# Softmax denominators of a convolution-attention layer: sums by accumulating DMAs, reciprocals with queries on partitions, stacking through DRAM

## The chip, the cores and the metric

The kernel runs on one core of one Trainium2 chip. The core has five engines that run their own instruction streams: PE (TensorE, matmuls and transposes), DVE (VectorE), ACT (ScalarE), POOL (GpSimd) and SP (SyncE, which here only issues DMAs). They share an on-chip memory of 128 partitions (SBUF), a small memory into which PE writes (PSUM), and 16 DMA engines. The metric is the device time of one execution in microseconds. Before the change the median of three runs is 3320.81 us (3317.92 to 3323.6).

## What is computed

Two layers work on x of shape 8 x 256 x 32 x 32 in float32. Layer 0 is a convolutional attention block with a feed-forward part, layer 1 a causal attention with a mixture of experts. The change lies in the attention of layer 0. For each of 8 images, with N = 1024 pixels and 4 heads with 32 channels in q and k and 64 in v:

```
qkv = _bn(_conv1x1(_ln(x), qkv_w))
q, k, v = qkv.reshape(B, NH, 2*KD + HD, N) split along the channels
attn = softmax(einsum('bhkn,bhkm->bhnm', q, k) * SCALE, axis=-1)
out  = einsum('bhdm,bhnm->bhdn', v, attn)
out  = out + _bn(_dwconv3(v))          # depthwise 3x3
x    = x + gamma1 * _bn(_conv1x1(out, proj_w))
x    = x + gamma2 * edffn(_ln(x))      # 1x1, depthwise 3x3, gelu gate, 1x1, 8x8 spectral filter
```

## The kernel before

Layer 0 keeps channels on partitions. The loop at the end of layer 0 runs over the images, one iteration for each. `together` takes two generators: `main_of(i)`, the attention of image i with the norms, the spectrum of image i-2 and the queries, keys and values of image i+1 woven in; and, beside it, `hidden(i-1)`, the depthwise convolutions of the image before, whose nine taps are mostly DVE instructions (`tap`). Every generator yields an estimate of its microseconds, and `together` takes steps of the second as long as its sum is behind the first's. So the order of the instructions on each engine is fixed when the program is built. All engines are wrapped by `InOrder` (line 69), which keeps that order; therefore nearly all instructions carry line 69 in the profile and are told apart by the tiles that they write and read.

`attend` (attention proper) computes transposed scores, keys on partitions. For a chunk c of QC = 256 queries and a key tile j of 128 keys, four chunks of eight steps each per image:

- PE writes the scores of four heads into `s` from the stacked keys `kst` and queries `qst`. A stack holds 4 x 32 rows per head: q and k are split into a part `hi`, rounded to a short mantissa for PE's faster float32 form (F32R), and the rest `lo`, and the rows are (hi, lo, hi, lo) for q and (hi, hi, lo, lo) for k.
- ACT takes the exponential into `pT` (128 keys x 4 heads x 256 queries, 512 KB), which has two buffers.
- One step later `product` multiplies with the transposed values `vT` into `po`: eight matmuls of 32 output columns each. Four more matmuls with `ones` add the exponentials over the keys into `sums` (the tile `sm`), which holds every head's sum on 32 partitions.

`close` ends a chunk. ACT copies `po` and the sums to SBUF (`pu`, `ss`), and a list of steps is run by `later`, one in each of the following steps: DVE takes the reciprocal of 128 x 256 (`sr`), ACT and POOL split it into `rh` and `rl`, four matmuls with `pick_r` spread it over the 64 channels of each head into `rb`, and DVE multiplies and adds to `o`. After the last chunk `finish` runs the same list, woven into `values` of the next image.

`queries_keys` makes `hi` and `lo` of queries (g = 0) and keys (g = 1), a pair of tiles for each; `stack` copies them into `qst` and `kst` with 32 DMAs of 128 KB from SP's queue (line 680), when the last scores of the image before have been taken. `values` and `project` run during that time. `rms_norm` sums squares on PE, then a chain of seven small POOL instructions takes the inverse root (`a`, `y`, `r`), PE transposes it (`tr`) and spreads it with `pick_n` (`rbn`).

The tiles `vpad` and `hpad` hold images with a border of zeros, 34 rows of 34. `vec` holds all per-channel vectors of both layers and is loaded by the first DMA. `accs` collects a check sum of the sums and reciprocals, by which the program decides at its end whether a safe form of layer 0 (`layer0_shifted`) has to be run; with these inputs it isn't.

PSUM is full: `ps_s` holds two buffers of `s` (four banks), `ps_o` one `po` and one `sums`, `ps_m` two buffers that all other products share.

Of the kernel before, what the change touches and what calls it, by code (L numbers as in the profile page):

```python
# [9 lines left out]
F32 = mybir.dt.float32  # L10
F32R = mybir.dt.float32r
# [7 lines left out]
P = 128  # L19
# [33 lines left out]
for _name, _w in _VEC:  # L53
    _VOFF[_name] = (_n, _w)
    _n += _w
NVEC = _n


# [16 lines left out]
def conv_attn_hybrid_kernel(  # L75
# [29 lines left out]

    vec = const.tile([P, NVEC], F32, name="vec")
    nc.sync.dma_start(vec, vecs)

    def col(name, i=0, n=1):
        o, w = _VOFF[name]  # L110
        assert i + n <= w
        return vec[:, o + i : o + i + n]

# [318 lines left out]
    with ExitStack() as l0:  # L432
# [3 lines left out]
        ps_s = l0.enter_context(tc.tile_pool(name="ps_s0", bufs=2, space=PSUM))  # L436
        ps_o = l0.enter_context(tc.tile_pool(name="ps_o0", bufs=1, space=PSUM))
        ps_m = l0.enter_context(tc.tile_pool(name="ps_m0", bufs=2, space=PSUM))
# [72 lines left out]
        for k in range(KC):  # L511
# [7 lines left out]

        pick_r = wpool.tile([P, NH // 2, P], F32R, name="pick_r")  # L520
        pickr = one.tile([P, NH, HD], F32, tag="full", name="pickr", bufs=2)
        nc.gpsimd.memset(pickr, 0.0)
        nc.gpsimd.affine_select(
            out=pickr, in_=pickr, compare_op=ALU.not_equal, fill=1.0, base=0,
            pattern=[[-KD, NH], [0, HD]], channel_multiplier=1,
        )
        nc.gpsimd.tensor_copy(pick_r.rearrange("p a (b c) -> p (a b) c", c=HD), pickr)

        nq = HALF // P
        pick_n = wpool.tile([2 * nq, nq, P], F32R, name="pick_n")  # L530
        pickn = one.tile([2 * nq, nq, P], F32, tag="full", name="pickn", bufs=2)
        nc.gpsimd.memset(pickn, 0.0)
        for half in range(2):
            nc.gpsimd.affine_select(
                out=pickn, in_=pickn, compare_op=ALU.not_equal, fill=1.0, base=-nq * half,
                pattern=[[-1, nq], [0, P]], channel_multiplier=1,
            )
# [8 lines left out]
        def padded(name):  # L546
            p = one.tile([P, H + 2, W + 2], F32, tag=name, name=name)
            nc.gpsimd.memset(p, 0.0)
            return p

        vpad = [padded(f"vpad{i}") for i in range(KC)]
        hpad = [padded(f"hpad{i}") for i in range(2)]

        def interior(p, h):
            r = H // 2
            return p[:, 1 + h * r : 1 + (h + 1) * r, 1 : 1 + W]

# [3 lines left out]
        def tap(dst, p, w, k):  # L561
            src = p[:, k // 3 : k // 3 + H, k % 3 : k % 3 + W]
            dve.scalar_tensor_tensor(rows(dst), src, w[:, k : k + 1], rows(dst), ALU.mult, ALU.add)
# [5 lines left out]
        def rms_norm(b, wname, xn):  # L569
# [38 lines left out]
            def apply(h):  # L608
                rT = rT_of.pop(h)
                rb = ps_m.tile([P, HALF], F32, tag="mm", name="rbn")  # L610
                for i in range(nq):
                    pe.matmul(rb[:, i * P : (i + 1) * P], pick_n[:, i, :], rT, start=True, stop=True)
# [39 lines left out]
        def queries_keys(b):  # L652

            att[b] = {"xn": one.tile([P, KC, N], F32, tag="xn", name="xn")}
            yield from rms_norm(b, "n1w", att[b]["xn"])
            for g in range(2):  # L660
                hi = one.tile([P, N], F32R, tag=f"hi{g}", name="hi")
                lo = one.tile([P, N], F32, tag=f"lo{g}", name="lo")
                bias = qkv_o[:, g : g + 1]

                def take(hs, pq):
                    act.activation(hi[:, hs], pq, AF.Identity, bias=bias)
                    dve.scalar_tensor_tensor(lo[:, hs], pq, bias, hi[:, hs].bitcast(F32), ALU.add, ALU.subtract)

                yield from qkv_group(b, g, take)
                att[b][g] = (hi, lo)  # L670

        def stack(b):
            for g in range(2):
                hi, lo = att[b][g]
                name = ("qst", "kst")[g]
                att[b][name] = st = one.tile([P, NH, N], F32R, tag=name, name=name)
                for r in range(4):
                    src = (hi, lo, hi, lo)[r] if g == 0 else (hi, hi, lo, lo)[r]
                    for hd in range(NH):
                        nc.sync.dma_start(  # L680
                            st[r * KD : (r + 1) * KD, hd, :].bitcast(F32), src[hd * KD : (hd + 1) * KD, :].bitcast(F32)
                        )

# [30 lines left out]
        def v_conv(b):  # L714
            o = att[b]["o"] = one.tile([P, KC, N], F32, tag="o", name="o")
            for g in range(KC):
                mid = vpad[g][:, 1 : 1 + H, 1 : 1 + W]
                act.activation(rows(o[:, g, :]), mid, AF.Identity, bias=pe_o[:, g : g + 1], scale=pe_w[:, g, 4:5])
            for g in range(KC):
                for k in OTHERS:  # L720
                    tap(o[:, g, :], vpad[g], pe_w[:, g, :], k)
                    yield 1.3

        def attend(b):
# [6 lines left out]

            def product(po, sm, j, pT):


                for pair in range(NH // 2):
                    for i in range(4):
# [7 lines left out]
                        )  # L744
                for hd in range(NH):
                    pe.matmul(
                        sm[hd * KD : (hd + 1) * KD, :], ones[:, :KD], pT[:, hd, :], start=(j == 0), stop=(j == nj - 1)
                    )

            def close(c, po, sm):  # L750
                pu = two.tile([P, NH // 2, QC], F32, tag="pu", name="pu", bufs=1)
                act.copy(pu, po)
                ss = two.tile([P, QC], F32, tag="ss", name="ss", bufs=1)
                act.activation(ss, sm, AF.Copy, accum_out=accs[:, 0, b, c : c + 1])
                r = two.tile([P, QC], F32, tag="sr", name="sr", bufs=1)
                rh = two.tile([P, QC], F32R, tag="rh", name="rh", bufs=1)
                rl = two.tile([P, QC], F32R, tag="rl", name="rl", bufs=1)
                qs = slice(c * QC, (c + 1) * QC)

                def invert():  # L760
                    dve.reciprocal(r, ss)

                def split():
                    act.activation(rh, r, AF.Copy, accum_out=accs[:, 1, b, c : c + 1])
                    pool.tensor_sub(rl, r, rh.bitcast(F32))
# [19 lines left out]
            for c in range(N // QC):  # L785
                qs = slice(c * QC, (c + 1) * QC)
                po = ps_o.tile([P, NH // 2, QC], F32, tag="po", name="po")
                sm = ps_o.tile([P, QC], F32, tag="sm", name="sums")
                for j in range(nj):
                    ks = slice(j * P, (j + 1) * P)  # L790
                    s = ps_s.tile([P, NH, QC], F32, tag="s", name="s")
                    for hd in range(NH):
                        pe.matmul(s[:, hd, :], kst[:, hd, ks], qst[:, hd, qs], start=True, stop=True)
                    pT = two.tile([P, NH, QC], F32, tag="pT", name="pT")
                    act.activation(pT, s, AF.Exp)
                    if late:
                        product(*late[:4])
                        if late[2] == nj - 1:
                            todo = close(c - 1, *late[:2])
                    late = (po, sm, j, pT)  # L800
                    later()
                    yield 1.75
            product(*late)
            todo = close(c, po, sm)
            att[b]["rest"] = todo
# [49 lines left out]
        def group_on_pe(b, n):  # L855
# [15 lines left out]
            for h in range(2):  # L871
                pc = ps_m.tile([P, HALF], F32, tag="mm", name="pc")
                for k in range(9):
                    r0 = h * r + k // 3
                    pe.matmul(
                        pc, diag[:, k, :], pad[:, r0 : r0 + r, k % 3 : k % 3 + W], start=(k == 0), stop=(k == 8)
                    )
                act.copy(dst[:, h * HALF : (h + 1) * HALF], pc)
# [911 lines left out]
```

## Time and profile before

| | |
|---|---|
| median of three runs | 3320.81 us |
| the profiled execution, time | 3326.09 us |
| the profiled execution, span | 3324.3 us |
| PE busy | 3108.8 us (94%) |
| DVE busy | 2395.9 us (72%) |
| ACT busy | 1417.6 us (43%) |
| POOL busy | 328.9 us (10%) |
| mean granted PE clock | 0.969 |
| layer 0 | 0 to about 1455 us |
| layer 1, attention | about 1455 to 2090 us |
| layer 1, experts | about 2090 to 3324 us |

The profile's slices show each engine's share in 40 pieces of 83 us, a digit for each. The groups of instructions give, for one operation on one set of tiles, the number of instructions, their busy time together, the mean of one in ns, and the idle time of the engine just ahead of them with what ended it. Instructions of PE overlap, so a group's busy time is smaller than count times mean. An fp32 matmul counts as two instructions, one in F32R as one. The windows give the busy time of each engine in a stretch of the execution.

### The profile page before, as it was taken

Reading aid. Unit: us, or ns where it says so; the run is one execution under the profiler, and the core shown is the slowest. Engines: PE = TensorE matmul, PEld = TensorE weight load, DVE = VectorE, ACT = ScalarE, POOL = GpSimd, SP = SyncE. Lnnn points to the kernel's source line nnn. Section 1 sums busy time; section 2 is a strip of 40 time slices with the busy share of each in tenths; the row PEclk is TensorE's granted clock in tenths of the full one; section 3 lists DMA queues with packets and bytes.
Section 4 is the critical chain, followed back from the end, with each engine's and each line's share of the span. In section 5 each row is a group of like instructions: output and inputs, shape, how many; then the busy total and the mean of one; then the engine's idle time right before and its main releaser. Section 6 shows DMA issues by size and latency. Waiting matters only on the chain.

```text
span 3324.3 us, 43278 instructions
## 1 busy us (share of the span) xinstructions
PE 3108.8 (94%) x17366; PEld 2108.0 (63%) x17366; DVE 2395.9 (72%) x3710; ACT 1417.6 (43%) x2185; POOL 328.9 (10%) x530
## 2 busy tenths in 40 slices
PE   6998999999999998769999998999999999999999
PEld 4554646464656555345556666687878777878787
DVE  2369788878787887744554444688888877888887
ACT  2545454555454544313333332344444444444443
POOL 1120101020202010001222222400000000000000
PEclk9989999999999999879999999899999999999999
DMA  4112020202020200030111101100000000000000
GB/s 121 29 24 51 26 52 26 51 27 51 27 51 26 52 14 7 16 134 13 51 47 43 39 26 45 45 25 21 20 20 20 24 18 26 23 20 26 13 7 13
DMA packets 42918, 113.85 MB, mean 34 GB/s; under 512 B 6406, under 2 KB 14550, under 8 KB 38870
## 3 DMA queue, kind: packets, MB, share of 16 engines
q1 hardware_dynamic: 42710, 111.01, 11.0%
q8 instruction: 139, 2.28, 0.3%
q14 instruction: 69, 0.57, 0.1%
HBM read 43.61 MB, written 33.82 MB: 23 GB/s over the span
## 4 chain that ended last, share of the span: by engine, by line
PE 50%; DVE 4%; ACT 1%; POOL 1%; issue 0%; DMA 0%; POOLq 0%; ACTq 0%; SPq 0%; DVEq 0%
PE pm L69 12%; PE pa L69 12%; PE q L69 11%; PE s L69 5%; PE po L69 3%; PE pv L69 2%; PE pk L69 2%; DVE zt L69 1%; DVE nm L69 1%; PE tpt L69 1%; DVE pr L69 1%; PE tp L69 1%; ACT pr L69 1%; PE tpz L69 1%; PE pw L69 1%
## 5 line engine op out<-in xcount | busy, mean ns | idle before, releaser
L69 ACT ACTIVATE h<-h,bn_o,bn_s 128x512 f32<-128x512 f32 x384 | 308.7, 813 | 632.5 <-DVE h L69 632.4
L69 DVE SCALAR_TENSOR_TENSOR conv<-hpad,vec,conv 128x1024 f32<-128x1024 f32 x256 | 331.4, 1300 | 14.7 <-ACT conv L69 8.9
L69 DVE SCALAR_TENSOR_TENSOR x<-hpad,vec,x 128x1024 f32<-128x1024 f32 x248 | 321.6, 1300 | 23.5 <-ACT x L69 17.4
L69 ACT ACTIVATE pT<-s 128x1024 f32<-128x1024 f32 x256 | 261.6, 1024 | 150.3 <-PE s L69 150.1
L69 PE MATMUL pm<-h,w 128*128 128x512 f32 (+1 forms) x768 | 318.1, 523 | 0.0
L69 PE MATMUL po<-pT,vT 128*32 128x256 f32 x4096 | 276.5, 388 | 6.5 <-ACT pT L69 4.8
L69 PE MATMUL ph<-xn,piw 128*128 128x512 f32 x512 | 246.1, 608 | 3.1 <-DVE gf L69 1.1
L69 PE MATMUL s<-kk,z 128*128 128x512 f32 x512 | 242.4, 601 | 0.6 <-DVE pr L69 0.6
L69 PE MATMUL s<-qst,kst 128*128 128x256 f32 x1024 | 217.9, 335 | 6.1 <-DMA kst<-lo 5.9
L69 PEld LDWEIGHTS s<-qst,kst 128*128 128x128 f32 x1024 | 147.8, 192 | 88.8 <-issue 72.2
L69 PEld LDWEIGHTS pm<-h,w 128*128 128x128 f32 x768 | 146.7, 191 | 75.6 <-issue 62.1
L69 DVE TENSOR_TENSOR h<-h,wb 128x1024 f32<-128x1024 f32 x128 | 156.8, 1225 | 43.2 <-ACT h L69 43.2
L69 DVE TENSOR_TENSOR h<-pa,first 128x512 f32<-128x512 f32 x128 | 88.3, 690 | 134.9 <-PE pa L69 131.4
L69 DVE SCALAR_TENSOR_TENSOR o<-vpad,pe_w,o 128x1024 f32<-128x1024 f32 x128 | 163.3, 1281 | 24.1 <-ACT o L69 21.2
L69 ACT ACTIVATE hpad<-ph,pi_o 128x512 f32<-128x512 f32 x126 | 87.0, 691 | 211.7 <-PE ph L69 207.2
L69 DVE TENSOR_TENSOR h<-h,first 128x256 f32<-128x256 f32 x384 | 164.3, 428 | 13.2
L69 PEld LDWEIGHTS po<-pT,vT 128*32 128x32 f32 x4096 | 107.7, 109 | 88.7 <-ACT pT L69 8.3
L69 PEld LDWEIGHTS ph<-xn,piw 128*128 128x128 f32 x512 | 90.8, 190 | 108.9 <-issue 92.1
L69 PE MATMUL sums<-pT,ones 128*32 128x256 f32 x2048 | 158.8, 382 | 0.0
L69 PE MATMUL pz<-pow__118,hid 128*128 128x256 f32 x512 | 129.8, 408 | 29.1 <-DVE hid L69 29.1
L69 PE MATMUL pa<-tz,ws 128*128 128x256 f32 x512 | 156.0, 387 | 0.0
L69 PE MATMUL pa<-ze,w 128*128 128x256 f32 x512 | 153.8, 383 | 0.0
(258 smaller groups left out, 5940.3 us busy)
## 6 DMA issues: line engine op xcount, KB each, us to landing
t<-in_x_dram SPq DMA_DIRECT2D x8, 1024.0 KB, 7.5
qst<-hi SPq DMA_DIRECT2D x64, 128.0 KB, 2.3
qst<-lo SPq DMA_DIRECT2D x64, 128.0 KB, 2.3
kst<-hi SPq DMA_DIRECT2D x64, 128.0 KB, 2.3
kst<-lo SPq DMA_DIRECT2D x64, 128.0 KB, 2.3
td<-t SPq DMA_DIRECT2D x8, 1024.0 KB, 3.8
t<-td SPq DMA_DIRECT2D x8, 1024.0 KB, 4.9
ze<-zd SPq DMA_DIRECT2D x16, 512.0 KB, 4.1
```

The lines of the kernel that those rows point to most:

```text
L69: return self._tc.keep_in_program_order(method(*args, **kwargs))
```

## The change

Four things change in layer 0, and some tiles get smaller.

1. `product` has no matmuls with `ones` any more. The exponentials of key tile 0 are written to a new tile `acc` in place of `pT`; those of each later tile are added to `acc` by a DMA that POOL issues with an adding operation. `pT` has three buffers and `acc` two. After the last tile, `total` makes the sums of a chunk with four matmuls on `acc`.
2. `close` no longer copies `po` to SBUF at once; `po` has two buffers. The sums are transposed (`turn`), so that queries lie on partitions and a reciprocal has 128 x 2 x 4 elements; POOL splits it into two parts (`rs`), PE transposes it back (`back`), two matmuls spread it (`spread`), ACT copies it to `pu`, and DVE multiplies with `po` (`divide`).
3. `hi` and `lo` have one buffer each for q and k together. SP writes them to DRAM (`part`) as soon as they are complete, and `stack` reads each stack with four DMAs from there, eight of 512 KB for an image in place of 32 of 128 KB.
4. `vec` is loaded in two parts, the second (`vec2`, the vectors of the experts) behind layer 0. `vpad` and `hpad` have rows of 33 elements, so that one column of zeros serves as the right border of a row and the left border of the next. `pick_n` is 8 x 4 and is widened by a stride of 0 in the matmul; `pick_r` is made for eight rows.

```
-        ps_o = l0.enter_context(tc.tile_pool(name="ps_o0", bufs=1, space=PSUM))
+        ps_o = l0.enter_context(tc.tile_pool(name="ps_o0", bufs=2, space=PSUM))
...
+            p = one.tile([P, (H + 2) * (W + 1) + 2], F32, tag=name, name=name)
...
+        def inside(p, r0, c0, h):
+            o = r0 * (W + 1) + c0
+            return p[:, o : o + h * (W + 1)].rearrange("p (h w) -> p h w", w=W + 1)[:, :, :W]
...
-                hi = one.tile([P, N], F32R, tag=f"hi{g}", name="hi")
-                lo = one.tile([P, N], F32, tag=f"lo{g}", name="lo")
+                hi = one.tile([P, N], F32R, tag="hi", name="hi")
+                lo = one.tile([P, N], F32, tag="lo", name="lo")
...
-                att[b][g] = (hi, lo)
+                parts = att[b][g] = [dram.tile([P, N], F32, tag=f"part{g}{r}", name="part", bufs=2) for r in range(2)]
+                for part, src in zip(parts, (hi, lo)):
+                    nc.sync.dma_start(part, src.bitcast(F32))
...
-                    for hd in range(NH):
-                        nc.sync.dma_start(
-                            st[r * KD : (r + 1) * KD, hd, :].bitcast(F32), src[hd * KD : (hd + 1) * KD, :].bitcast(F32)
-                        )
+                    nc.sync.dma_start(
+                        st[r * KD : (r + 1) * KD].bitcast(F32), src.rearrange("(h k) n -> k h n", k=KD)
+                    )
...
-                for hd in range(NH):
-                    pe.matmul(
-                        sm[hd * KD : (hd + 1) * KD, :], ones[:, :KD], pT[:, hd, :], start=(j == 0), stop=(j == nj - 1)
-                    )
+                if j:
+                    pool.dma_start(acc, pT, accum_op=ALU.add)
...
+                def total():
+                    sm = ps_m.tile([P, QC], F32, tag="mm", name="sums")
+                    for hd in range(NH):
+                        pe.matmul(sm[hd * KD : (hd + 1) * KD, :], ones[:, :KD], acc[:, hd, :], start=True, stop=True)
+                    ss = of["ss"] = two.tile([P, QC], F32, tag="ss", name="ss", bufs=1)
+                    act.activation(ss, sm, AF.Copy, accum_out=accs[:, 0, b, c : c + 1])
+
+                def turn():
+                    tp = ps_m.tile([P, nt, P], F32, tag="mm", name="tps")
+                    for i in range(nt):
+                        pe.transpose(tp[:, i, :], of["ss"][:, i * P : (i + 1) * P], ident)
+                    r = small.tile([P, nt, NH], F32, tag="sr", name="sr", bufs=2)
+                    dve.reciprocal(r, tp[:, :, ::KD])
+                    flat = r.rearrange("p a b -> p (a b)")
+                    act.activation(flat, flat, AF.Copy, accum_out=accs[:, 1, b, c : c + 1])
+                    rs = of["rs"] = small.tile([P, nt, 2, NH], F32, tag="rsp", name="rs", bufs=2)
+                    pool.tensor_copy(rs[:, :, 0, :].bitcast(F32R), r)
+                    pool.tensor_sub(rs[:, :, 1, :].bitcast(F32R), r, rs[:, :, 0, :])
+
+                def back():
+                    tr = ps_m.tile([2 * NH, QC], F32, tag="mm", name="trs")
+                    for i in range(nt):
+                        pe.transpose(tr[:, i * P : (i + 1) * P], of["rs"][:, i].rearrange("p a b -> p (a b)"), ident)
+                    of["rT"] = small.tile([2 * NH, QC], F32R, tag="rsT", name="rsT", bufs=2)
+                    act.copy(of["rT"], tr)
+
                 def spread():
                     rb = ps_m.tile([P, NH // 2, QC], F32, tag="mm", name="rb")
                     for pair in range(NH // 2):
-                        pe.matmul(rb[:, pair, :], pick_r[:, pair, :], rh, start=True, stop=False)
-                        pe.matmul(rb[:, pair, :], pick_r[:, pair, :], rl, start=False, stop=True)
+                        pe.matmul(rb[:, pair, :], pick_r[:, pair, :], of["rT"], start=True, stop=True)
+                    pu = of["pu"] = two.tile([P, NH // 2, QC], F32, tag="pu", name="pu", bufs=1)
+                    act.copy(pu, rb)
+
+                def divide():
+                    pu = of["pu"]
+                    dve.tensor_mul(pu, po, pu)
                     o = att[b]["o"][:, :, qs]
-                    dve.tensor_mul(pu, pu, rb)
                     dve.tensor_add(o, o, pu)
...
-                return [None, invert, None, split, None, None, spread]
+                return [None, None, total, turn, None, back, spread, divide]
...
+                acc = two.tile([P, NH, QC], F32, tag="acc", name="acc")
...
-                    pT = two.tile([P, NH, QC], F32, tag="pT", name="pT")
+                    pT = two.tile([P, NH, QC], F32, tag="pT", name="pT", bufs=3) if j else acc
...
+    more.append(wm.tile([P, NVEC - NVEC0], F32, name="vec2"))
+    nc.sync.dma_start(more[0], vecs[:, NVEC0:])
```

More of the change, by code (lines that the diff above doesn't have):

```diff
@@ L56 @@
 NVEC = _n
+NVEC0 = _VOFF["b1"][0]
 class InOrder:
@@ L104, in conv_attn_hybrid_kernel @@
     small = ctx.enter_context(tc.tile_pool(name="small", bufs=4))
-    vec = const.tile([P, NVEC], F32, name="vec")
-    nc.sync.dma_start(vec, vecs)
+    vec = const.tile([P, NVEC0], F32, name="vec")
+    nc.sync.dma_start(vec, vecs[:, :NVEC0])
+    more = []
     def col(name, i=0, n=1):
@@ L111, in col @@
         assert i + n <= w
+        if o >= NVEC0:
+            return more[0][:, o - NVEC0 + i : o - NVEC0 + i + n]
         return vec[:, o + i : o + i + n]
@@ L517, in conv_attn_hybrid_kernel @@
         nc.vector.tensor_mul(dw_o, pi_o, dw_w[:, :, 4])
-        pick_r = wpool.tile([P, NH // 2, P], F32R, name="pick_r")
-        pickr = one.tile([P, NH, HD], F32, tag="full", name="pickr", bufs=2)
+        pick_r = wpool.tile([2 * NH, NH // 2, P], F32R, name="pick_r")
+        pickr = one.tile([2 * NH, NH, HD], F32, tag="full", name="pickr", bufs=2)
         nc.gpsimd.memset(pickr, 0.0)
-        nc.gpsimd.affine_select(
-            out=pickr, in_=pickr, compare_op=ALU.not_equal, fill=1.0, base=0,
-            pattern=[[-KD, NH], [0, HD]], channel_multiplier=1,
-        )
+        for half in range(2):
+            nc.gpsimd.affine_select(
+                out=pickr, in_=pickr, compare_op=ALU.not_equal, fill=1.0, base=-NH * half,
+                pattern=[[-1, NH], [0, HD]], channel_multiplier=1,
+            )
         nc.gpsimd.tensor_copy(pick_r.rearrange("p a (b c) -> p (a b) c", c=HD), pickr)
         nq = HALF // P
-        pick_n = wpool.tile([2 * nq, nq, P], F32R, name="pick_n")
-        pickn = one.tile([2 * nq, nq, P], F32, tag="full", name="pickn", bufs=2)
+        pick_n = wpool.tile([2 * nq, nq], F32R, name="pick_n")
+        pickn = one.tile([2 * nq, nq], F32, tag="full", name="pickn", bufs=2)
         nc.gpsimd.memset(pickn, 0.0)
@@ L535, in conv_attn_hybrid_kernel @@
                 out=pickn, in_=pickn, compare_op=ALU.not_equal, fill=1.0, base=-nq * half,
-                pattern=[[-1, nq], [0, P]], channel_multiplier=1,
+                pattern=[[-1, nq]], channel_multiplier=1,
             )
@@ L546, in padded @@
         def padded(name):
-            p = one.tile([P, H + 2, W + 2], F32, tag=name, name=name)
+            p = one.tile([P, (H + 2) * (W + 1) + 2], F32, tag=name, name=name)
             nc.gpsimd.memset(p, 0.0)
             return p
+        def inside(p, r0, c0, h):
+            o = r0 * (W + 1) + c0
+            return p[:, o : o + h * (W + 1)].rearrange("p (h w) -> p h w", w=W + 1)[:, :, :W]
         vpad = [padded(f"vpad{i}") for i in range(KC)]
@@ L554, in interior @@
         def interior(p, h):
-            r = H // 2
-            return p[:, 1 + h * r : 1 + (h + 1) * r, 1 : 1 + W]
+            return inside(p, 1 + h * (H // 2), 1, H // 2)
         def rows(ap):
@@ L561, in tap @@
         def tap(dst, p, w, k):
-            src = p[:, k // 3 : k // 3 + H, k % 3 : k % 3 + W]
+            src = inside(p, k // 3, k % 3, H)
             dve.scalar_tensor_tensor(rows(dst), src, w[:, k : k + 1], rows(dst), ALU.mult, ALU.add)
@@ L611, in apply @@
                 for i in range(nq):
-                    pe.matmul(rb[:, i * P : (i + 1) * P], pick_n[:, i, :], rT, start=True, stop=True)
+                    pe.matmul(
+                        rb[:, i * P : (i + 1) * P], pick_n[:, i : i + 1].to_broadcast([2 * nq, P]), rT, start=True, stop=True
+                    )
                 hs = slice(h * HALF, (h + 1) * HALF)
@@ L678, in stack @@
                     src = (hi, lo, hi, lo)[r] if g == 0 else (hi, hi, lo, lo)[r]
-                    for hd in range(NH):
-                        nc.sync.dma_start(
-                            st[r * KD : (r + 1) * KD, hd, :].bitcast(F32), src[hd * KD : (hd + 1) * KD, :].bitcast(F32)
-                        )
+                    nc.sync.dma_start(
+                        st[r * KD : (r + 1) * KD].bitcast(F32), src.rearrange("(h k) n -> k h n", k=KD)
+                    )
         def values(b):
@@ L716, in v_conv @@
             for g in range(KC):
-                mid = vpad[g][:, 1 : 1 + H, 1 : 1 + W]
+                mid = inside(vpad[g], 1, 1, H)
                 act.activation(rows(o[:, g, :]), mid, AF.Identity, bias=pe_o[:, g : g + 1], scale=pe_w[:, g, 4:5])
@@ L730, in attend, with product @@
             todo = []
-            def product(po, sm, j, pT):
+            def product(po, acc, j, pT):
                 for pair in range(NH // 2):
@@ L744, in product @@
                         )
-                for hd in range(NH):
-                    pe.matmul(
-                        sm[hd * KD : (hd + 1) * KD, :], ones[:, :KD], pT[:, hd, :], start=(j == 0), stop=(j == nj - 1)
[L748 to L757, printed above, removed]
-                qs = slice(c * QC, (c + 1) * QC)
[L760 to L765, printed above, removed]
+                if j:
+                    pool.dma_start(acc, pT, accum_op=ALU.add)
@@ new lines, in close @@
+            def close(c, po, acc):
+                qs = slice(c * QC, (c + 1) * QC)
+                nt = QC // P
+                of = {}
+                def total():
[21 more added lines that the diff above has]
+                    act.copy(of["rT"], tr)
@@ L787, in attend @@
                 po = ps_o.tile([P, NH // 2, QC], F32, tag="po", name="po")
-                sm = ps_o.tile([P, QC], F32, tag="sm", name="sums")
+                acc = two.tile([P, NH, QC], F32, tag="acc", name="acc")
                 for j in range(nj):
@@ L793, in attend @@
                         pe.matmul(s[:, hd, :], kst[:, hd, ks], qst[:, hd, qs], start=True, stop=True)
-                    pT = two.tile([P, NH, QC], F32, tag="pT", name="pT")
+                    pT = two.tile([P, NH, QC], F32, tag="pT", name="pT", bufs=3) if j else acc
                     act.activation(pT, s, AF.Exp)
                     if late:
-                        product(*late[:4])
-                        if late[2] == nj - 1:
+                        product(*late)
+                        if j == 0:
                             todo = close(c - 1, *late[:2])
-                    late = (po, sm, j, pT)
+                    late = (po, acc, j, pT)
                     later()
@@ L803, in attend @@
             product(*late)
-            todo = close(c, po, sm)
+            todo = close(c, po, acc)
             att[b]["rest"] = todo
@@ L874, in group_on_pe @@
                     r0 = h * r + k // 3
-                    pe.matmul(
-                        pc, diag[:, k, :], pad[:, r0 : r0 + r, k % 3 : k % 3 + W], start=(k == 0), stop=(k == 8)
-                    )
+                    pe.matmul(pc, diag[:, k, :], inside(pad, r0, k % 3, r), start=(k == 0), stop=(k == 8))
                 act.copy(dst[:, h * HALF : (h + 1) * HALF], pc)
```

## The prediction

> **What bounds the kernel now.** I read the page's totals and slices first, then one layer-0 iteration as windows, then the matmul groups, the exponentials in order of time, and the DMA rows.
>
> ```profile
> PE 3108.8 (94%) x17366; PEld 2108.0 (63%) x17366; DVE 2395.9 (72%) x3710; ACT 1417.6 (43%) x2185; POOL 328.9 (10%) x530
> PE   6998999999999998769999998999999999999999
> DVE  2369788878787887744554444688888877888887
> DMA  4112020202020200030111101100000000000000
> ```
>
> Slices 1 to 15 (83 us each) are layer 0: PE at nine tenths, DVE at seven or eight, the DMA engines almost idle. What PE issues in order sets the time. The chain of waits starts only at 1452 us, behind layer 0, so it says nothing here.
>
> ```profile
> 508.70:672.40 163.70, 154.82 (x1230) 91.06 (x1229) 135.75 (x129) 85.12 (x130) 20.97 (x33) 0.98 0.15 40
> 508.70:551.00 42.30, 40.53 (x316) 26.18 (x315) 35.06 (x39) 16.00 (x23) 8.57 (x13) 1.00 0.10 35
> 635.00:672.40 37.40, 32.34 (x123) 18.65 (x116) 34.85 (x35) 22.77 (x36) 3.07 (x3) 0.91 0.48 109
> ```
>
> One iteration (columns: window, length, then busy PE, PE loads, DVE, ACT, POOL, clock, DMA share, GB/s): PE works 154.8 of 163.7 us, DVE 135.8. In the last 37 us, after the 32 attention steps, the DMA share is 0.48: the stacking. POOL is busy 21 us and issues no DMA.
>
> ```profile
> L69 PE MATMUL po<-pT,vT 128*32 128x256 f32 x4096 | 276.5, 388 | 6.5 <-ACT pT L69 4.8 <-ACT pu L69 1.6
> L69 PE MATMUL sums<-pT,ones 128*32 128x256 f32 x2048 | 158.8, 382 | 0.0
> L69 PE MATMUL s<-qst,kst 128*128 128x256 f32 x1024 | 217.9, 335 | 6.1 <-DMA kst<-lo 5.9
> L69 PE MATMUL tpv<-ident,vfull 128*128 128x128 f32 x128 | 20.7, 285 | 19.1 <-ACT vfull L69 17.2 <-ACT conv L69 1.0 <-DVE pu L69 0.9
> L69 PE MATMUL rb<-rh,pick_r 128*128 128x256 f32 x64 | 22.9, 374 | 18.1 <-ACT rh L69 17.3 <-ACT vT L69 0.8
> L69 PE MATMUL rb<-rl,pick_r 128*128 128x256 f32 x64 | 20.3, 333 | 3.3 <-POOL rl L69 3.3
> L69 PE MATMUL tr<-ident,r 128*8 128x128 f32 x32 | 9.2, 286 | 6.2 <-ACT conv L69 4.8 <-POOL r L69 1.4
> ```
>
> The sums cost PE 158.8 us, 0.62 in each of 256 steps. The waits of po (6.5) and s (6.1, of it 5.9 once, for the first stack) are small: neither a second po buffer nor faster stacking has much to win.
>
> **What goes.** The sums stay only once per chunk: 7/8 of 158.8 = 139.0 us of PE removed. Half of the rb matmuls go: (22.9 + 20.3)/2 = 21.6. Added are, per chunk, two transposes of 128 columns and two of 8: 64 of each. The tpv row is 64 transposes (128 instructions) for 20.7; of the narrow kind the tr row gives 9.2/32 = 0.29 per instruction when isolated, so 20.7 to 36.8; I take 28.8. Net 139.0 + 21.6 - 20.7 - 28.8 = **111 us of PE at most**, 14 per iteration. On DVE 32 reciprocals of 128x256 (1.75 us each, 56 in all) become tiny ones; that lies beside PE and counts nothing, unless DVE is the bound, where 7 us per iteration would count. ACT still copies 128x512 once per chunk (0.59).
>
> **What comes.** Each chunk of 8 steps gets 7 accumulating DMAs of 512 KB, SBUF to SBUF, issued by POOL. All seven write the same acc, so each must wait for the landing of the one before: they are a chain. Let D be its cycle; an iteration has 28 of them. The trace has no such transfer. The nearest rows:
>
> ```profile
> kst<-lo SPq DMA_DIRECT2D x64, 128.0 KB, 2.3
> td<-t SPq DMA_DIRECT2D x8, 1024.0 KB, 3.8
> out_dram<-te SPq DMA_DIRECT2D x16, 512.0 KB, 2.8
> 633.00:656.00 23.00, 18.58 (x96) 9.38 (x96) 20.66 (x21) 17.05 (x27) 0.84 (x1) 0.92 0.81 183
> ```
>
> (DMA rows: KB of one, us from issue to landing.) Lower end: a plain 512 KB write, 2.8 us. For SBUF to SBUF: while the 32 stack DMAs run, 183 GB/s at a share of 0.81, so 226 GB/s when full. 128 KB take 0.58 of the 2.3, which leaves 1.7 fixed; 512 KB take 2.3, so a plain copy is 4.0. The accumulation also reads acc: between nothing and another 2.3; I take half, 1.15. Issue on POOL: small POOL instructions show what DVE does to them:
>
> ```profile
> 672.25 1.76 POOL L69 TENSOR_TENSOR y<-y,a 128x4 f32<-128x4 f32 x2
> 674.10 1.23 POOL L69 TENSOR_SCALAR y<-y 128x4 f32<-128x4 f32 x1
> 582.29 0.19 POOL L69 TENSOR_SCALAR y<-y 128x4 f32<-128x4 f32 x1
> ```
>
> The same 128x4 operation takes 0.19 us or 1.23, the length of the tap that DVE runs beside it. So the wait and issue on POOL add 0.35 (SP's issue of a large DMA) to 1.25; I take 0.35. **D = 1.7 + 2.3 + 1.15 + 0.35 = 5.5 us, between 2.8 and 1.7 + 2.3 + 2.3 + 1.25 = 7.6.**
>
> The Trainium skill ("DMA: Bandwidth & Descriptors", Anatomy of one DMA — SWDGE (gpsimd) path) fits a POOL-issued DMA as about 2.0 us plus its bytes at 436 GB/s; an estimate from that page is 3.2 us for 512 KB, and 4.4 if the read of acc counts as bytes too, which would put the time near 3370 us. The skill's "SBUF — State Buffer" (Who interferes with whom) says that a DVE instruction with two SBUF inputs contends with GpSimd reads; the 0.19 against 1.23 agrees. It adds that generating descriptors is blocked only by DVE's two-port modes, which by itself would favour the low end; no row here shows it.
>
> **Where D meets the steps.** In the iteration at 508.7 the exponentials (one per step) start at 508.7, 513.3, 519.7, 525.3, 536.8, 544.1, 548.7, 550.1; then the chunks of 31.5, 27 and 27 us; the last at 633.2; the next iteration's first at 672.4, 39.2 later. Bare steps are 2.1 apart. Three pT buffers let ACT run at most three DMAs ahead, so chunks two to four, which need 7 x 5.5 = 38.5, are set by the chain. The first chunk (42.3 long, steps 0.6 shorter now) starves the chain twice; walked through with D = 5.5, its seventh DMA lands 50 us after the first step. Then 21 x 5.5 = 115.5, so the last lands at 165.5. In finish, total makes PE wait for that landing; queued behind it on PE are values, ph and project. Of the 39.2 about 11 (the rest of the last step and three woven steps) lie ahead of total, so 28 remain: 193.5 against 163.7, **+30**.
>
> - Iterations 2 to 6: 5 x 30 = 150.
> - Iteration 7 (115.3 from first to last exponential, then 39.2 = 154.5): 193.5 - 154.5 = +39.
> - Iteration 1 (186.6 to 342.5 = 156; its steps are dense, the chain never starves): 5 + 28 x 5.5 + 28 = 187, +31.
> - Iteration 0 (73.7 to 186.6 = 113, gap 33.5): 5 + 154 + 22 = 181, +68.
>
> Sum **+288**. The 14 us saved on PE per iteration vanish inside this.
>
> **Edits at about nothing.** Stacking by DRAM: four writes and eight 512 KB reads for 32 DMAs of 128 KB (0.62 us of SP each, 20 us). The cover is values and project: the last DMA is issued 21 us after the first, the next step comes 15 us later. At the start there is no cover, PE waits 5.9; the new way adds a write (2.8) and saves issue: between -6 and +6, I take -3. One hi and lo for q and k: k's first half (620.7) comes 5.9 after q's last (614.8), the write takes 2.8 to 3.1: hidden; without that gap it would cost 3 per iteration. SP's queue gets these ahead of the t store and load, tens of us early. POOL's norm chain (a, y, r) now queues behind waiting DMAs; behind it PE's tr waits, up to one D. Under a binding chain that costs nothing, since a DMA is in flight meanwhile; where the chain does not bind, POOL hardly waits. The second load of vec adds one SP issue (0.4) ahead of layer 1: +1. Rows of 33, the shrunk pick_n and the smaller vec change no operation's size.
>
> Against the profiled run (span 3324.3, time 3326.1): 3326 + 288 - 3 + 1 = 3612. That run lies 5 above the median of 3320.8, so I forecast **3607 us**.
>
> **The rivals.**
>
> - *A, the chain keeps up*: D under about 3.9, as if the read of acc were hidden and POOL's issue inside the 1.7. For it: the plain 512 KB row of 2.8, idle DMA engines. Against: 2R1W for a 1R1W row, and SBUF-to-SBUF traffic of only 226 GB/s. With D = 3.2 iterations 2 to 7 are PE's and gain 14 each (84), iteration 1 gains 10, iteration 0 loses 4 (5 + 90 + 22 = 117 for 113): 3321 - 90 - 3 = **3228**. With all 111 it would be 3207; DVE, then about 129 of 150 us, may take half back, 3265. It decides below D = 4.0, where the gain has just gone.
> - *B, POOL and both reads at full price*: D = 7.6, descriptors stretched by the taps as the 1.23 us rows are. Every chunk is the chain's: 5 + 213 + 28 = 246 in iterations 1 to 7, 240 in 0: 82 x 5 + 91 + 90 + 127 = +718, **4037**.
> - *C, the accumulations are not serialised by waits*: then D is the transfer alone, 2.3 to 4.6, and the time is A's or just above no change. Against: seven read-modify-writes of one tile need the order; I give it a part of A.
>
> **Chances.** Forecast (D 4.3 to 6.8, which by the same walk is 3360 to 3855): 0.57. A with C: 0.22. B: 0.18. Around no change: 0.03. About 0.2% is what a measurement of this kernel can tell from none. So faster 0.21, same 0.03, slower 0.76. The range runs from inside A (3290, D near 3.8) to nearly B (3990, D near 7.4), leaving about 0.1 out on each side.
>
> **What would show it.** Right: POOL's DMA rows 5 to 6 us from issue to landing; ACT's pT waiting for a DMA; chunks of 38 us whatever else is woven in; PE near seven tenths in layer 0 and waiting in sums for the last accumulation; an iteration of about 193 us; layers behind 1455 us unchanged but shifted. Wrong: landings of 3 us or less with PE still at nine tenths (A), POOL issue above 1 us each (B), or iterations long while pT never waits for a DMA, which none of these explains.

## The result and the profile after

The changed kernel takes 3650.86 us (median of four runs, 3646.58 to 3658.82); the kernel before took 3320.36 beside it. The ratio is 1.0997 (95% interval 1.0974 to 1.1021): 330 us slower, where 3607 us was forecast. The profiled execution took 3658.82 us, its span is 3657.1.

The page of the changed kernel, totals and slices (now 91 us each):

```profile
PE 3112.3 (85%) x15638; PEld 2083.0 (57%) x15638; DVE 2337.6 (64%) x3710; ACT 1429.6 (39%) x2218; POOL 533.2 (15%) x787
PE   5657686877877786767599999889999999999999
PEclk9868898998888897989799999979999999999999
DMA  4645647374646455440301001110000000000000
```

PE falls from nine tenths to six to eight in layer 0 and nowhere else; the DMA engines go from nearly idle to about half. The granted clock falls in layer 0 too. All the time is in layer 0: its end (the load of `at`) moves from 1452.7 to 1779.7 us, by 327.

Groups of the changed kernel and two of its waits (the waits: who waited for what, us in total, times, longest):

```profile
L70 POOL DMA_DIRECT2D acc<-pT x224 | 195.1, 899 | 982.5 <-DMA acc<-pT 720.5
L70 PE MATMUL po<-pT,vT 128*32 128x256 f32 x3584 | 263.2, 415 | 73.8 <-ACT pT L70 73.8
L70 ACT ACTIVATE pT<-s 128x1024 f32<-128x1024 f32 x224 | 228.1, 1024 | 240.5 <-DMA acc<-pT 156.6
L70 PE MATMUL sums<-acc,ones 128*32 128x256 f32 x256 | 33.5, 614 | 264.1 <-DMA acc<-pT 264.1
```

```profile
POOL acc L70 <- DMA acc<-pT: 720.5, 148, 14.1
PE sums L70 <- DMA acc<-pT: 264.1, 32, 19.2
```

All of them lead back to one releaser, the landing of an accumulating DMA: POOL waits for it to issue the next (148 of 224 times), ACT to write `pT`, PE behind ACT in `po`, and PE in every one of the 32 `sums`.

The DMA issues of the changed kernel (KB of one, us to landing), the queue that carries the accumulating DMAs (packets, MB, share of the time of the 16 engines), and POOL's queue in order of time in the iteration that starts at 462.4 us:

```profile
acc<-pT POOLq DMA_DIRECT2D x224, 512.0 KB, 4.6
qst<-part SPq DMA_DIRECT2D x32, 512.0 KB, 10.0
kst<-part SPq DMA_DIRECT2D x32, 512.0 KB, 18.2
q0 software_dynamic: 32256, 117.45, 16.9%
```

```profile
478.76 0.86 POOL L70 DMA_DIRECT2D acc<-pT  x1 [5.71 <-DMA acc<-pT]
483.85 0.86 POOL L70 DMA_DIRECT2D acc<-pT  x1 [4.22 <-DMA acc<-pT]
...
605.31 0.86 POOL L70 DMA_DIRECT2D acc<-pT  x1 [5.22 <-DMA acc<-pT]
618.82 0.86 POOL L70 DMA_DIRECT2D acc<-pT  x1 [12.65 <-ACT vfull L70]
631.03 0.86 POOL L70 DMA_DIRECT2D acc<-pT  x1 [11.35 <-DMA acc<-pT]
```

From one issue to the next a link, one accumulating DMA of the chain, takes 5.09 us where nothing disturbs it (478.76 to 483.85): 4.6 to landing, the rest until POOL issues again. Where a chunk ends, the first link of the next one writes the other buffer of `acc` and doesn't wait: at 511.85 POOL issues two within 1.74 us. Of the image's last three links two take 13.5 and 12.2 us. SP issued the eight stack loads of the next image at 603 to 609, so both share the DMA engines; the name ACT vfull in one bracket is that of an instruction which ended nearby; what POOL waits for there is, as in its neighbours, the landing. What PE does meanwhile, and the same stretch as windows (length; busy PE, PE loads, DVE, ACT, POOL; clock; DMA share; GB/s):

```profile
617.80 0.60 PE L70 MATMUL tpv<-ident,vfull 128*128 128x128 f32 x4
635.73 1.08 PE L70 MATMUL sums<-acc,ones 128*32 128x256 f32 x8 [17.32 <-DMA acc<-pT]
```

```profile
617.00:636.00 19.00, 1.68 (x11) 0.87 (x13) 7.37 (x8) 3.75 (x6) 1.72 (x2) 0.68 0.84 173
636.00:645.00 9.00, 6.49 (x24) 3.29 (x17) 3.66 (x5) 4.79 (x11) 1.14 (x2) 0.50 0.00 0
```

PE idles 17.3 us for one sum and then runs at half clock: the eight matmuls of a sum take 1.08 us, where the kernel before took 0.61.

### The profile page after: what moved, and what is told of

The parts are those of the page before. It is cut to its first block, busy times and chain, and to the rows that moved or that the text cites. A ratio compares the mean times of both kernels' runs of the same rounds, so it can differ in the third digit from the quotient of the medians.

```text
span 3657.1 us, 40101 instructions
## 1 busy us (share of the span) xinstructions
PE 3112.3 (85%) x15638; PEld 2083.0 (57%) x15638; DVE 2337.6 (64%) x3710; ACT 1429.6 (39%) x2218; POOL 533.2 (15%) x787
## 3 DMA queue, kind: packets, MB, share of 16 engines
q0 software_dynamic: 32256, 117.45, 16.9%
## 4 chain that ended last, share of the span: by engine, by line
PE 45%; DVE 3%; ACT 1%; POOL 1%; issue 0%; DMA 0%; SPq 0%; ACTq 0%; POOLq 0%; DVEq 0%
PE pm L70 11%; PE pa L70 11%; PE q L70 10%; PE s L70 4%; PE po L70 3%; PE pv L70 2%; PE pk L70 2%; DVE zt L70 1%; DVE nm L70 1%; PE tpt L70 1%; DVE pr L70 1%; PE tp L70 1%; ACT pr L70 1%; PE tpz L70 0%; PE pw L70 0%
## 5 line engine op out<-in xcount | busy, mean ns | idle before, releaser
L70 POOL DMA_DIRECT2D acc<-pT x224 | 195.1, 899 | 982.5 <-DMA acc<-pT 720.5
L70 PE MATMUL po<-pT,vT 128*32 128x256 f32 x3584 | 263.2, 415 | 73.8 <-ACT pT L70 73.8
L70 ACT ACTIVATE pT<-s 128x1024 f32<-128x1024 f32 x224 | 228.1, 1024 | 240.5 <-DMA acc<-pT 156.6
L70 PE MATMUL ph<-xn,piw 128*128 128x512 f32 x512 | 262.7, 643 | 5.8 <-DVE gf L70 3.3
L70 PE MATMUL sums<-acc,ones 128*32 128x256 f32 x256 | 33.5, 614 | 264.1 <-DMA acc<-pT 264.1
L70 PE MATMUL s<-qst,kst 128*128 128x256 f32 x1024 | 237.2, 358 | 13.5 <-DMA kst<-part 13.5
L70 PEld LDWEIGHTS s<-qst,kst 128*128 128x128 f32 x1024 | 161.8, 211 | 107.9 <-issue 103.7
L70 PEld LDWEIGHTS po<-pT,vT 128*32 128x32 f32 x3584 | 98.6, 115 | 159.7 <-ACT pT L70 86.0
L70 DVE TENSOR_TENSOR h<-h,first 128x256 f32<-128x256 f32 x384 | 164.3, 428 | 13.2
```

The source lines that it names most:

```text
L70: return self._tc.keep_in_program_order(method(*args, **kwargs))
```

## The experiments

All times are medians beside the kernel before, which took 3320 to 3323 us in these runs; ratios to it have their 95% interval in brackets.

**The accumulations left out.**

```
-                if j:
-                    pool.dma_start(acc, pT, accum_op=ALU.add)
```

> The changed kernel without its 224 accumulating DMAs: the exponentials of key tiles 1 to 7 are left out of the denominators, all else stays. Theory (the serial chain of accumulations, with its last links, costs everything): PE alone sets layer 0 again with the sums gone, 3321 minus up to 111, so 3205 to 3260 us, and PE's wait ahead of sums is gone. Rival 1 (the other parts cost: waits of the new close, stacking by way of DRAM): 3321 or more. Rival 2 (DVE takes over as the bound): 3265 to 3310.

3294.6 us, 0.9914 (0.9897 to 0.993). The chain costs 3650.9 - 3294.6 = 356 us, more than the whole loss of 330; without them the rest of the change is no loss. But the time is that of rival 2: with free accumulations the change would have gained 29 us, not 111. More on this below.

**The last three links of each image left out** (key tiles 5 to 7 of the fourth chunk).

```
+                if j and not (last_chunk() and j > nj - 4):
                     pool.dma_start(acc, pT, accum_op=ALU.add)
```

> The changed kernel without the last three accumulations of the fourth chunk of each image (key tiles 5 to 7 left out of those denominators). In the changed kernel's trace these last links take 12 to 13 us each, beside the stack's loads, and PE waits 17.3 us for the last. Theory that both the chain inside the chunks and this tail cost: the stretch from the last exponential to the next image's first falls from 55 to about 40 us and the time by 8 x 15 = 120, to 3510 to 3550. Rival (the tail is nearly the whole loss): 3320 to 3380. Rival (the gap is the stack's own and not the tail's): 3620 or more.

3547.6 us, 1.0669 (1.0651 to 1.0687): 103 less. In images 2 to 6 the next image's first exponential comes 41 to 42 us after the last one, for 54 to 57. So about 13 us an image are the price of these last links (the tail), and the other 253 of the 356 belong to the chain inside the chunks.

**Everything but the accumulating DMAs, and the stacking alone.** The first keeps the sums on PE in the changed kernel, with `po` in one buffer and copied out as soon as a chunk ends; the second puts only the DRAM stacking into the kernel before.

```
+                for hd in range(NH):
+                    pe.matmul(sm[hd * KD : (hd + 1) * KD, :], ones[:, :KD], pT[:, hd, :], start=(j == 0), stop=(j == nj - 1))
-                if j:
-                    pool.dma_start(acc, pT, accum_op=ALU.add)
...
+                act.copy(pu, po)
```

> Everything of the change but the accumulating DMAs: sums by four matmuls per step as before, po with one buffer copied out at once, reciprocals with queries on partitions, stacks by way of DRAM. Theory: close to the kernel before, plus the new transposes less half of the rb matmuls, 28 us of PE at most: 3310 to 3350. Rival 1 (the other parts cost): 3420 or more.

> The kernel before with nothing but the new stacking (one hi and one lo, four writes to DRAM, eight loads of 512 KB). Theory: hidden behind values and project, 3310 to 3330. Rival 1: the loads land late (18 us in the changed kernel) and the first scores of each image wait for them, 3360 or more.

3329.7 us, 1.0021 (1.0011 to 1.003), and 3330.4 us, 1.002 (1.001 to 1.0029). They lie 6 and 7 us above before, so the stacking accounts for it and the new reciprocals for nothing measurable (`po` in two buffers, held until `divide`, isn't in these two). The stacking's price is a single wait, at the very start, of PE for the first stack, 13.2 us for 5.9 before:

```profile
L69 PE MATMUL s<-qst,kst 128*128 128x256 f32 x1024 | 215.9, 334 | 13.2 <-DMA kst<-part 13.2
```

**Copies in place of accumulations**, from POOL and from SP (only the last key tile reaches the denominators).

```
-                    pool.dma_start(acc, pT, accum_op=ALU.add)
+                    pool.dma_start(acc, pT)
```

> The changed kernel with plain copies on POOL's queue in place of the accumulating ones: same 512 KB, same chain, each overwrites acc, so only the last key tile is in the denominators. Prices the reading of acc, taken as 1.15 us of D. Theory: a copy lands about 1.1 us sooner than the 4.6 of the accumulating DMA, near 3.5, and the time falls by some 200 us per us of D, to 3400 to 3480. Rival (the cycle is fixed cost of a POOL-issued DMA, the add is free): 4.4 to 4.6, 3620 to 3660.

> The same plain copies, issued by SP (only the last key tile is in the denominators). Prices POOL's issue: 0.86 us against SP's 0.35. Theory: lands 0.4 to 0.6 us sooner than the copy from POOL and the time is 80 to 120 us lower than that run's. Rival (the issue is not in the chain): the same time within 20 us. The copies stand in SP's queue ahead of the stacking, which may cost some of it.

3435.3 us, 1.0343 (1.0324 to 1.0362), and 3342.9 us, 1.0057 (1.0037 to 1.0077). The issues and the share of the DMA engines, first of the copies from POOL, then from SP:

```profile
q0 software_dynamic: 32256, 117.45, 8.8%
acc<-pT POOLq DMA_DIRECT2D x224, 512.0 KB, 2.9
```

```profile
acc<-pT SPq DMA_DIRECT2D x224, 512.0 KB, 2.9
kst<-part SPq DMA_DIRECT2D x32, 512.0 KB, 13.9
```

A copy lands after 2.9 us, the accumulation after 4.6: accumulating costs 1.7 us of the link, where 1.1 was expected (the run can't tell the second read from the addition). The time falls by 216 us, 127 for each us of landing and not the 200 assumed. On the engines it doubles the work: 16.9% of 3657 us over 224 are 2.76 us of all sixteen, 8.8% of 3433 are 1.35. The Trainium skill ("Collectives: The Full Stack", The bandwidth ceiling: the fold count and why AG ≠ RS ≠ AR) says of collective operations that a reducing transfer takes two source reads through the same ring and so runs at half a copy's rate; here, within one core, the 2.76 against 1.35 agree.

SP's copies came out 92 us lower, inside the 80 to 120 expected, but not for the reason given: both copies land after 2.9, none sooner. The larger part is SP's order: the copies stand ahead of the stack loads in one queue and no longer run beside them, and the gap after an image's last exponential is 42 us, for 49 with POOL's copies. The seven gaps together are 58 of the 88 us by which layer 0 ends sooner (1468.6 for 1556.7). Inside the chunks it is 34 us. There POOL's copies also stand behind POOL's other work (the split of the reciprocals waited 172 us for ACT in the run with POOL's copies), and no run separates that from the length of the issue.

**Two accumulators.** Tile 0 takes tiles 1, 2, 5, 7, tile 3 takes 4 and 6; `total` reads both.

```
+                if j in (1, 2, 5, 7):
+                    pool.dma_start(accs_[0], pT, accum_op=ALU.add)
+                elif j in (4, 6):
+                    pool.dma_start(accs_[1], pT, accum_op=ALU.add)
```

> Two accumulators a chunk: tile 0 takes tiles 1, 2, 5, 7, tile 3 takes 4 and 6; total reads both (eight matmuls); pT has two buffers in place of three to stay in memory. 192 accumulating DMAs of the same size; the longest chain has four links for seven. Theory (serial latency is the bound, the engines carry 2.8 us each): chunks are no longer the chain's, what is left is the tail beside the stack's loads: 3380 to 3500. Rival (the DMA engines' throughput or POOL's issue is the bound): 192/224 of the loss stays, 3590 to 3640.

3437.9 us, 1.0353 (1.0335 to 1.0372): 213 less with 192 transfers for 224 of the same kind (4.7 us to landing). The rival's 3590 to 3640 is far off, so neither the engines' throughput nor POOL's issue sets the loss, but the order in series. Still, the gain isn't all the chunks', and what is left isn't the tail's, as was expected. The gap between images is back at 42 us, as in the run without accumulations, because the last two links no longer stand one behind the other: in image 3 POOL issues them at 697.8 and 701.1 us, as the stack loads begin, and `sums` waits 1.6 us. Over the seven gaps that is 87 us. From first to last exponential, summed over the eight images, the time is 1017 us, for 1141 in the changed kernel and 880 without accumulations: inside the chunks two chains win back 124 of 261 us. There ACT now waits 194.5 us for landings that free `pT`, for 156.6; how much of that is its two buffers in place of three was not tried.

**Sums shared between DMA and PE** (tiles 1, 3 and 5 by DMA).

```
+                if j in (1, 3, 5):
+                    pool.dma_start(acc, pT, accum_op=ALU.add)
+                for part in ([pT] if j and j not in (1, 3, 5) else []) + ([acc] if j == nj - 1 else []):
```

> The sums shared out: tiles 1, 3 and 5 are accumulated into tile 0 by DMA, tiles 2, 4, 6, 7 and the accumulator are summed on PE (5 groups of four matmuls a chunk for 8), close as in the run with all sums on PE. Theory: three links of 5.1 us end long before the chunk does and none meets the stack's loads, so PE gains 3 x 0.43 us x 32 chunks = 41 against that run's 3330: 3285 to 3305, below both kernels. Rival (any accumulating DMA costs more than the matmuls it saves): 3325 or more.

3350.1 us, 1.0085 (1.0071 to 1.0099): a miss. From the first exponential of image 2 to that of image 7 it takes 817.8 us, before 822.4, so three eighths of the sums away are worth about 1 us an image:

```profile
372.90:1190.70 817.80, 768.42 (x5702) 448.23 (x5701) 642.87 (x642) 429.93 (x661) 167.30 (x242) 0.96 0.40 91
```

PE's work did fall by the 5 us an image that were expected, if its busy time is taken times the mean clock (768.4 x 0.96 = 738; before 778.0 x 0.98 = 762). The lower clock (30 us lost, for 16) and idle time (49 for 44) took back nearly all of it. The first two images, where bare steps of 2.1 us meet links of 5.1, lose 24 us (79.8 to 372.9 against 73.7 to 342.5), and 6 are lost at the start.

**The stack loads behind the last links**, issued by POOL.

```
-                    nc.sync.dma_start(
+                    pool.dma_start(
                         st[r * KD : (r + 1) * KD].bitcast(F32), src.rearrange("(h k) n -> k h n", k=KD)
```

> The changed kernel with the eight stack loads of an image issued by POOL, behind the last accumulations in its queue, in place of SP, whose loads run beside them. Theory (the last links are slow, 12 to 13 us, because they share the DMA engines with the stack's loads): the last links fall back to about 5 us, PE's wait for them shrinks by some 12 us an image and the time falls by 60 to 100, to 3550 to 3590, unless the first scores then wait for a later stack. Rival (the last links are slow for another reason): 3630 or more.

3565.0 us, 1.0731 (1.0709 to 1.0753): 86 less by issuing the same loads behind the links. PE's wait in `sums` falls from 264.1 to 169.9 us:

```profile
PE sums L70 <- DMA acc<-pT: 169.9, 32, 7.9
```

POOL issues the last links of image 2 5.0 to 5.7 us apart (577.53 to 593.33), the gap between images is 41 to 42 us from image 2 on, and the first scores wait no longer than in the changed kernel. So most of the tail's price, 86 of 103 us, is the collision.

**A later total.**

```
-                return [None, None, total, turn, None, back, spread, divide]
+                return [None, None, None, None, total, turn, back, both]
```

> The changed kernel with the steps of close moved: total in the fifth step of the next chunk in place of the third, the others behind it, spread and divide together in the eighth. PE's 264 us of waiting in sums for the last accumulation are the largest wait of the profile. Theory (the chain's length is the bound, the wait in sums only shows it): the wait moves to pT, and to product behind it, inside the chunks; 3600 to 3660. Rival (total stands too early, and that is the loss): 3400 to 3500.

3653.3 us, 1.0995 (1.0957 to 1.1033): no change. A wait and two groups of this kernel:

```profile
ACT pT L70 <- DMA acc<-pT: 287.1, 96, 8.4
```

```profile
L70 PE MATMUL po<-pT,vT 128*32 128x256 f32 x3584 | 279.2, 435 | 80.5 <-ACT pT L70 80.1
L70 PE MATMUL sums<-acc,ones 128*32 128x256 f32 x256 | 25.9, 484 | 79.1 <-DMA acc<-pT 79.1
```

PE's wait in `sums` falls from 264 to 79, ACT's for the same landings rises from 157 to 287 and PE's behind it, in `po`, from 74 to 80. The largest wait of a profile was only where the chain came to light.

**Without accumulations and with half the feed-forward taps on DVE.**

> The run without accumulations (3294.6), and on top of it every second tap of the feed-forward convolutions on DVE left out (about 250 of 1.3 us, 320 us of DVE): both the sums and those taps are missing from the output. Asks why 111 us less of PE gave only 29. Theory (PE is still the bound, at a lower granted clock, 0.92 in layer 0 for 0.95): within 40 us, 3255 to 3295. Rival (DVE took over): 3150 to 3230.

3233.2 us, 0.9723 (0.9697 to 0.975): 61 below the run without accumulations, for 315 us less of DVE. The time lies between the two expectations, 3 us above the rival's range. DVE isn't the bound, but a fifth of its time comes back; over the same five images of this run (775.9 us from first exponential to first exponential, for 810.4) PE is busy 731.0 us at a mean clock of 0.96. So about the same PE work (702 us at full clock) is left, and of the 34.5 us half is idle time of PE (45 us, for 62) and half its higher clock.

## Why the prediction was right, and where it was off

**The mechanism** was as put: seven dependent accumulations a chunk, three buffers of slack, and a chain that outlasts the steps. Of the signs named for it, ACT's and PE's waits and the shifted layers behind came as put, and an iteration took 199.3 us for about 193. The landings are 4.6 us, not 5 to 6. The chunks are not 38 us each: in the iteration at 462.4 they start 43, 40 and 28 us apart, 110.5 together; 21 links of 5.1 are 107. In the first, POOL waited twice for `pT` (7.8 and 7.1 us) and not for a landing. The images, from first exponential to first exponential (before, after, difference, forecast):

| image | before | after | difference | forecast |
|---|---|---|---|---|
| start | 73.7 | 81.0 | +7 | -3 |
| 0 | 112.9 | 183.1 | +70 | +68 |
| 1 | 156.0 | 198.3 | +42 | +31 |
| 2 to 6, each | 164.5 | 199.3 | +35 | +30 |
| 7, to layer 1 | 287.8 | 320.9 | +33 | +40 |

**D** was 5.1, forecast 5.5. Two terms were mis-sized against each other. The plain copy was put at 4.0, by the rate of the copies that fill 32 partitions; the copy over 128 partitions landed in 2.9. The read of `acc` was put at half a transfer, 1.15; accumulating cost 1.7. What lies between a landing and the next issue is 0.5, for 0.35. POOL's issue is 0.86 us long in the median and 1.21 at most, so the taps hardly stretch it: rival B's ground fell away.

**The walk** through the chunks had two more steps wrong. It counted the links of neighbouring chunks in series (21 x 5.5 behind the first chunk), though the two buffers of `acc` let them overlap at each chunk's end. And it left out that the links queue behind POOL's norm chain: at 460.1 to 471.6 that chain runs, and the image's first link is issued at 472.1, 4.2 us after its `pT` was written.

**The tail** was missed. The walk let the last link land 165.5 us after the first exponential, at undisturbed links; it landed at 635.7 - 462.4 = 173.3, since stack loads and last links were each costed as if alone. The runs without the tail (103 us) and with the loads behind it (86) are the price. The two slow links exceed 5.1 us each by 15 together (13.5 + 12.2 - 10.2). That an iteration still came out near the forecast is luck: the smaller D, 28 times 0.4 or 11 us, and the overlaps at the chunks' ends worked against that.

**The stacking** was taken at -3 and cost 7, just above its upper bound of +6: in the prologue nothing hides it, and the issue time that it saves is of no use there. In the run with the stacking alone SP has issued the eight loads by 63.5 us, but the DMA engines stay full from 58 to 78 (share 1.04) and move 6.3 MB, for 4.2 before, since the writes come on top. Elsewhere the cover that was named held.

**Rival A** had the wrong price. It took PE's removed time, 14 us an image, at face value; the run without accumulations gained 2.4 an image where the steps are woven (810.4 for 822.4 us over five images) and 29 in all. Windows over these five images, before and without accumulations:

```profile
342.50:1164.90 822.40, 778.00 (x6148) 457.63 (x6147) 674.78 (x638) 425.27 (x642) 102.61 (x160) 0.98 0.15 39
```

```profile
326.44:1136.82 810.38, 748.18 (x5062) 433.11 (x5061) 641.32 (x642) 432.42 (x661) 107.29 (x181) 0.93 0.20 53
```

At full clock PE's work falls from about 778.0 x 0.98 = 762 to 748.2 x 0.93 = 696 us, some 13 an image, as computed (the mean clocks have two digits, so 1 to 2 us an image are open). Of that the lower clock takes some 7 (748 - 696 = 52 us lost, for 16) and idle time 3.5 (62 us for 44). Why it idles more is seen in the run's PE timeline:

```profile
545.12 1.07 PE L70 MATMUL po<-pT,vT 128*32 128x256 f32 x16 [1.26 <-ACT pT L70]
...
549.50 1.94 PE L70 MATMUL po<-pT,vT 128*32 128x256 f32 x16
...
562.43 1.07 PE L70 MATMUL po<-pT,vT 128*32 128x256 f32 x16
```

The sums had filled PE's time while ACT took the exponential. Without them PE waits, and then the same sixteen instructions take 1.94 us for 1.07. The run with fewer taps shows that the idle time added here goes with DVE's taps (45 us of idle are left, 44 before), and that the clock rises with it (0.96 for 0.93). That the clock takes the rest follows from these windows; no run changed the clock by itself.

## What to carry to other kernels

Work taken off a busy engine and given to idle DMA engines must be costed as latency: a read-modify-write chain runs at one link per landing (5.1 us here), however idle the engines are; two chains won back about half of what one lost inside the chunks (124 of 261 us). Ask what each new transfer runs beside: moving eight loads behind the image's last links was worth 86 us. And price a removal on the engine that bounds by what is left to fill its waits, not by the busy time that goes.

## What the runs showed of the hardware

PE's granted clock can drop to half after short waits. After the 1.26 us above it fell, within 3 us, to 0.50, though PE had not waited longer in the 40 us before:

```profile
549.00:552.00 3.00, 3.00 (x21) 1.37 (x20) 0.27 (x1) 1.76 (x3) 2.32 (x7) 0.50 0.00 0
```

The Trainium skill ("TensorE: Matmul & The Clock Gate", What's actually happening) puts the drop after an idle window of about 3.4 us; here 1.26 was enough, and the measurement decides. The length of the wait alone doesn't settle it. In the same run waits of 1.49 us (at 163.8) and 1.45 (at 1169.3) were followed by no drop for 13 us and more. In the kernel before, one wait of 0.83 us (at 566.0) was followed by none, another just as long (at 1056.9) by a mean clock of 0.63 from 1061 to 1064. What decides was not found. In layer 0 the mean clock is 0.85 in the changed kernel and 0.95 before; with it PE's busy time there stays the same, 1308 us, although the sums lost 125 of their 159.

An accumulating DMA issued by POOL occupies it for 0.86 us, a copy for 0.53. And a link of 5.1 us, issue to issue, became one of 12.2 and one of 13.5 beside eight plain loads of the same size from another queue.
